# Two graph-attention layers on one core: half of a block's product moved into the next block's sums, and a GpSimd memset between two gathers

## The chip, the core and the metric

The kernel runs on one core of one Trainium2 chip. The metric is the device time of one execution in microseconds (us); the time before is a median of three runs. A profile is a separate execution, in which the hardware profiler records every instruction; its times are read against each other, and its span is longer than the timed runs.

## What is computed

The input is a matrix `x` of 2708 nodes by 1024 features and an adjacency matrix `adj` of 2708 x 2708 with few ones in a row (the kernel keeps at most 40 neighbours of a node). Two attention layers follow each other, each with a residual and a layer norm. Layer 0 scores a pair of nodes by a product of two projections, layer 1 by the sum of two numbers of the nodes:

```python
# layer 1; x is the output of layer 0
h = x @ W
f1 = h @ a1
f2 = h @ a2
e = leaky_relu(f1 + f2.T, negative_slope=0.2)
scores = where(adj > 0, e, -9e15)
attention = softmax(scores, axis=1)
x = layernorm(x + relu(attention @ h), axis=-1)
```

All of it is in float32.

## The kernel before

*Lists, not matrices.* A first stage turns each row of `adj` into a list of neighbours (`lists`, L402 on), sorts the nodes by the length of their lists and makes 22 blocks of them: one of 20 nodes, and 21 of 128 nodes each, a block being four groups of 32 nodes. A group with lists of up to 4 T entries has T *tiles*: a tile is 128 rows of 1024 features (in layer 1 and its ring, 1028: one more column holds a score), four neighbours of each of 32 nodes, fetched from memory by one indirect DMA, a *gather*, which GpSimd issues. There are 405 tiles in a layer; the first block has 3, most of the others 20.

*The order of layer 1.* `(attention @ x) @ W` is computed instead of `attention @ (x @ W)`. For each block `b` the loop at L1007 writes down, in this order:
- the copies (ScalarE) of the last block's turned rows, `yT`;
- the **sums** of block `b` (L679): for every tile, two matmuls (one for each half of 512 columns) add weighted rows into the PSUM tile `po`; four matmuls on the four column groups of the array run side by side. `st` holds the weights. When both halves of a tile are done, its slot is free and `gathers()` (L642) issues the next gathers, in program order, for as long as freed slots allow. At the end ScalarE copies `po`, divided by the row sums `ri`, into `y`;
- the **product** of block `b - 1` (`product`, L533): 16 matmuls `yT @ M`, 8 for each half of 512 columns, into the PSUM tile `pm`. In the records each matmul of float32 is two, so a product has 32;
- eight transposes (`turn`, L515) of `y` of block `b`, into the PSUM tile `pt`;
- the **close** of block `b - 2` (`close1`, L994): VectorE reads `pm`, adds the residual, and takes the norm; ScalarE applies it; GpSimd scatters the rows to the output (from a hook inside the next sums);
- the **scores** of block `b + 1` (`scores1`, L976): VectorE adds the column of scores in the gathered tiles to a number of each node, takes the maximum, ScalarE the exponential, and VectorE spreads the result into `st`.

*What holds the order.* Every engine gets its instructions through `InOrder` (L61), which keeps them in the order in which the program writes them; engines wait for each other by semaphores only.

*Buffers.* Gathered tiles live in a ring of 32 slots (20 in `ring`, 12 in `more`), so a gather waits until the tile 32 places earlier has been summed. `pm` has two buffers, `po` one, `y` and `yT` one each. A gather also waits for the eighth GpSimd DMA before it, since these share eight semaphores.

The helpers record all these operations under L71, so the groups are told apart by their tiles.

Of the kernel before, what the change touches and what calls it, by code (L numbers as in the profile page):

```python
# [8 lines left out]
F32 = mybir.dt.float32  # L9
# [97 lines left out]
def listed_path(ctx, tc, x, adj, Wf, bf, Wg, bg, W, bW, W1, a1, a2, out):  # L107

    nc = tc.nc
    P = 128  # L110
    N, D = x.shape
    KC = D // P
    H = D // 512
    TW = D + 4
# [6 lines left out]
    start = [0] + [valid[0] + P * b for b in range(NB - 1)]  # L121
# [11 lines left out]
    pe, dve, act, pool, sp = (InOrder(tc, e) for e in (nc.tensor, nc.vector, nc.scalar, nc.gpsimd, nc.sync))  # L133
# [5 lines left out]
    ps_m = ctx.enter_context(tc.tile_pool(name="ps_m", bufs=2, space=bass.MemoryType.PSUM))  # L139
# [3 lines left out]
    T1 = dram.tile([N, TW], F32, name="T1")  # L143
# [6 lines left out]
    ones3 = const.tile([35, P], BF16, name="ones3")  # L150
# [23 lines left out]
    rows3 = const.tile([35, D], BF16, name="rows3")  # L174
# [5 lines left out]
    def gather(engine, dst, table, idx, rows=N):  # L180
        engine.indirect_dma_start(
            out=dst, out_offset=None, in_=table,
            in_offset=bass.IndirectOffsetOnAxis(ap=idx, axis=0), bounds_check=rows - 1, oob_is_err=False)
# [3 lines left out]
    M = wm.tile([P, KC, D], F32, name="M")  # L187
# [6 lines left out]
    with tc.tile_pool(name="pre", bufs=1) as pre:  # L194
# [292 lines left out]
        for b in range(NB):  # L487
            n = nsize[b]
            pe.matmul(pt[:64, 0, :NG], low4[:n, b].rearrange("p j i -> p (j i)"), hot[:n, b, :],
                             start=(b == 0), stop=(b == NB - 1))  # L490
# [42 lines left out]
    def product(n, xT, w, row=None):  # L533


        pm = ps_m.tile([P, H, 512], F32, name="pm")
        for h in range(H):
            c = slice(h * 512, (h + 1) * 512)
            if row is not None:
                pe.matmul(pm[:n, h, :], ones3[row:row + 3, :n], rows3[row:row + 3, c], start=True, stop=False)  # L540
            for k in range(KC):
                pe.matmul(pm[:n, h, :], xT[:, k, :n], w[:, k, c],
                          start=(row is None and k == 0), stop=(k == KC - 1))
        return pm

    def split_product(xT, w, parts, row=None):

# [78 lines left out]
    class Layer:  # L626

        def __init__(self, units, rings, width, table, stp):  # L630
            self.units, self.table, self.width, self.stp = units, table, width, stp
            self.slots = [(t, i) for t in rings for i in range(t.shape[1])]
            self.count = len(self.slots)
            self.order = [(u, g, t) for u in units for _, g, t in u.tiles]
            assert self.count <= sum(TILES[:NSL0])
            self.next, self.free, self.most = 0, set(), len(self.order)
# [5 lines left out]
        def gathers(self):  # L642
            while self.next < min(self.most, len(self.order)) and (self.next < self.count or self.next - self.count in self.free):
                u, g, t = self.order[self.next]
                idx = SL[:, g, t:t + 1] if self.next >= self.count else SL0[:, g, t:t + 1]
                gather(pool, self.rows(self.next), self.table, idx)
                self.next += 1

        def soft(self, u):
# [93 lines left out]
    ring = ctx.enter_context(tc.tile_pool(name="ring", bufs=1)).tile([P, R0, TW], F32, name="ring")  # L743
    with ExitStack() as s0s:
# [3 lines left out]
        stp, xp, yp, jp = (new_pool(n, 1) for n in ("stp0", "xp", "yp", "jp0"))  # L748
        zs = new_pool("zp", 1).tile([P, TW], F32, name="z")
        seq = [1, 0, *range(2, NB)]  # L750
        units = cut(R0, 2, seq)
        lay = Layer(units, [ring], D, x, stp)
# [124 lines left out]
        closing, loaded = iter(()), None  # L877
# [77 lines left out]
    with ExitStack() as s1s:  # L955
        new_pool = lambda name, bufs: s1s.enter_context(tc.tile_pool(name=name, bufs=bufs))
        tp, yp, zp, ovp = (new_pool(n, 1) for n in ("tp1", "yp1", "zp1", "ovp"))
        stp = new_pool("stp1", 2)

        x1 = [rb, u1b]  # L960
        z1 = [u2b, zp.tile([P, D], F32, name="z1")]
        more = new_pool("ring1", 1).tile([P, R1 - R0, TW], F32, name="more")
        units = cut(R1, Q, range(NB))
        lay = Layer(units, [ring, more], TW, T1[:, :], stp)
        prod, yTs, y = {}, {}, {}


        fq = ovp.tile([P, NB, Q], F32, name="fq")
        f1q = ovp.tile([P, NB, Q], F32, name="f1q")
        dve.tensor_tensor(fq, f1.unsqueeze(2).to_broadcast([P, NB, Q]), quad.unsqueeze(1).to_broadcast([P, NB, Q]),  # L970
                          op=ALU.mult)
        pt = ps_t.tile([P, 4, P], F32, name="pt")
        pe.matmul(pt[:, 0, :Q * NB], rep, fq.rearrange("p b q -> p (b q)"), start=True, stop=True)
        dve.tensor_copy(f1q.rearrange("p b q -> p (b q)"), pt[:, 0, :Q * NB])

        def scores1(u):  # L976
            for k, g in enumerate(u.gs):
                at = [lay.slots[(u.at + m) % lay.count] for m, tile in enumerate(u.tiles) if tile[0] == k]
                t0 = 0
                while t0 < len(at):  # L980

                    t, s = at[t0]
                    step = at[t0 + 1][1] - s if t0 + 1 < len(at) and at[t0 + 1][0] is t else 0
                    c = 1
                    while step > 0 and t0 + c < len(at) and at[t0 + c][0] is t and at[t0 + c][1] == s + c * step:
                        c += 1
                    dve.tensor_scalar(u.sc[:, k, t0:t0 + c], t[:, s:s + (c - 1) * step + 1:max(step, 1), D],
                                      f1q[:, u.b, k:k + 1], None, op0=ALU.add)
                    t0 += c
            dve.scalar_tensor_tensor(u.sc, u.sc, SLOPE, u.sc, op0=ALU.mult, op1=ALU.max)  # L990
            dve.tensor_add(u.sc, u.sc, masked(u))
            lay.soft(u)

        def close1(b):  # L994
            m, xt, z = valid[b], x1[b % 2], z1[b % 2]
            sp.dma_start(xt[:m], X1S[start[b]:start[b] + m, :])
            dve.scalar_tensor_tensor(z[:m], flat(prod.pop(b))[:m], 0.0, xt[:m], op0=ALU.max, op1=ALU.add)
            for _ in norm(z, m):
                pass
            yield  # L1000
            scatter(out, ids[:m, b:b + 1], z[:m])

        lay.gathers()
        scores1(units[0])
        closing = iter(())
        waiting = []
        for k, u in enumerate(units):  # L1007
            nxt = units[k + 1] if k + 1 < len(units) else None
            b = u.b
            back = b - 1 if b > 0 else None  # L1010
            po = ps_s.tile([P, H, 512], F32, name="po")
            y[b] = yp.tile([P, D], F32, name="y1")
            if back is not None:
                for _ in yTs[back][1]:
                    pass
            lay.sums(u, po, {6: [lambda s=closing: [None for _ in s]]}, y[b])
            closing = iter(())
            if back is not None:
                if back > 0:
                    prod[back] = product(P, yTs.pop(back)[0], M)  # L1020
                else:
                    prod[back] = whole(split_product(yTs.pop(back)[0], M, z1[1]))
            yT = tp.tile([P, KC, P], F32, name="yT")
            steps = turn(y.pop(b), nrows[b], yT, halves=True)
            next(steps)
            yTs[b] = yT, steps
            if waiting:
                closing = close1(waiting.pop())
                next(closing)
            if back is not None:  # L1030
                waiting.append(back)
            if nxt is not None:
                scores1(nxt)
        for _ in closing:
            pass
        b = NB - 1
        for _ in yTs[b][1]:
            pass
        prod[b] = product(nrows[b], yTs.pop(b)[0], M)
        for b in waiting + [b]:  # L1040
            for _ in close1(b):
                pass


        over = ovp.tile([P, NG, QT], F32, name="over")
        pool.memset(over, 0.0)
        for g in range(1, NG):
            if TILES[g] < QT:
                pool.memset(over[:, g, TILES[g]:], 1.0)
        for q in range(Q):  # L1050
            pool.memset(over[32 * q:32 * q + valid[0], 0, TILES[0]:], 1.0)
        dve.scalar_tensor_tensor(over, SL, float(N), over, op0=ALU.is_lt, op1=ALU.mult)
        dve.tensor_reduce(bad[:, 0:1], over, AX.XY, ALU.add)
        dve.tensor_reduce(bad[:, 0:1], bad, AX.X, ALU.add)
        pt = ps_t.tile([P, 4, P], F32, name="pt")
        pe.matmul(pt[0:1, 0, 0:1], bad[:, 0:1], ones, start=True, stop=True)
        act.copy(flag, pt[0:1, 0, 0:1])
# [365 lines left out]
```

## Time and profile before

The time before is 1823.62 us (1822.46 to 1825.52). The profiled execution has a span of 2002.7 us.

| In the profile | busy us, or number | share of the span |
|---|---|---|
| TensorE (PE), matmuls | 1664.6 | 83% |
| VectorE (DVE) | 1174.9 | 59% |
| ScalarE (ACT) | 634.7 | 32% |
| GpSimd (POOL) | 1191.8 | 60% |
| gathers of layer 1 into `ring` | 260, mean 1003 ns | 260.9 us busy |
| gathers of layer 1 into `more` | 145, mean 1005 ns | 145.7 us busy |
| records of products `pm<-M,yT` | 704, mean 661 ns | 361.9 us busy |
| records of sums `po<-ring,st` and `po<-more,st` | 2660 and 580 | 346.7 and 88.2 us busy |

How to read it: a row of an engine is the time in which it executes something, not the time in which it is needed. A line of a timeline gives the start, the duration, the engine, the source line, the operation with its tile names (output `<-` inputs), the count, and in brackets how long the engine was idle before it and what released it; "issue" stands for nothing that the profile shows, "remote" for a releaser that it can't name. Columns of a table by stage are the stage, its length, the busy time (and number of instructions) of each engine, then the granted clock of TensorE as a share of full speed, the busy share of the 16 DMA engines, and the rate in GB/s.

The first gather of layer 1 starts at 1244.74 us of the span. In the 100 us from 1600 on TensorE is busy for 82.95 us and GpSimd for 62.41; the mean over the whole span hides that the stages differ.

### The profile page before, as it was taken

The page shows a single profiled execution, that of the slowest core. Times are in us where ns is not written, and L with a number is a line of the kernel's source. Part 1 is how long each engine was busy: PE and PEld are TensorE (multiplying, and loading weights), DVE is VectorE, ACT ScalarE, POOL GpSimd, SP SyncE. Part 2 cuts the span into 40 slices and gives each one's busy share as a digit, 9 for nine tenths or more (in the row PEclk, how much of TensorE's full clock was granted, in tenths as well). Part 3 has the DMA queues.
Part 4 walks back from the last instruction along what each step waited for, and adds up shares of the span by engine and source line. Part 5 has one row for each costly group of instructions (what it writes and reads, how often), then busy time and mean ns, then how long its engine had stood idle before and what let it go on. Part 6 is the DMA issues. An engine that isn't in the chain of part 4 may idle for free. (4 is left out here: it accounts for less than half of the span.)

```text
span 2002.7 us, 22908 instructions
## 1 busy us (share of the span) xinstructions
PE 1664.6 (83%) x7313; PEld 683.8 (34%) x7313; DVE 1174.9 (59%) x3541; ACT 634.7 (32%) x857; POOL 1191.8 (60%) x1191
## 2 busy tenths in 40 slices
PE   5998556899999889999999975468788888887985
PEld 3443222333344333443434432123233333332332
DVE  5879465788888678888888863123232323232332
ACT  4546134444554444445554440011010101011111
POOL 6978445666676456665666531755656565766621
PEclk9999677999999899999999988688889888998988
DMA  6644354656778567876777753887889889998830
GB/s 262 240 170 176 119 220 164 228 199 242 268 285 299 207 226 256 291 258 243 279 277 272 270 215 114 351 298 269 319 300 328 297 306 318 337 330 317 297 145 33
DMA packets 149982, 501.85 MB, mean 251 GB/s; under 512 B 32566, under 2 KB 32598, under 8 KB 147145
## 3 DMA queue, kind: packets, MB, share of 16 engines
q0 software_dynamic: 132032, 427.36, 59.7%
q1 hardware_dynamic: 10202, 55.72, 7.5%
q10 hardware_dynamic: 7618, 17.23, 2.4%
q8 instruction: 59, 0.97, 0.2%
q14 instruction: 71, 0.57, 0.1%
HBM read 509.64 MB, written 33.75 MB: 271 GB/s over the span
## 5 line engine op out<-in xcount | busy, mean ns | idle before, releaser
L71 POOL DMA_INDIRECT ring<-in_x_dram,SL x405 | 437.2, 1079 | 318.6 <-issue 97.0
L71 DVE SCALAR_TENSOR_TENSOR j<-ring,Fr 128x1024 bf16<-128x1024 f32 x402 | 494.8, 1231 | 89.4 <-DMA ring<-in_x_dram,SL 60.2
L71 PE MATMUL pm<-M,yT 128*128 128x512 f32 (+1 forms) x704 | 361.9, 661 | 85.7 <-issue 84.5
L71 POOL DMA_INDIRECT ring<-T,SL x260 | 260.9, 1003 | 166.3 <-issue 58.8
L71 PE MATMUL po<-ring,st 128*32 128x512 f32 x2660 | 346.7, 619 | 6.3 <-issue 6.2
L71 ACT COPY Fr<-pm 32x1024 f32<-32x1024 f32 (+1 forms) x349 | 338.4, 970 | 27.1 <-issue 16.3
L71 PE MATMUL pm<-M,xT 128*128 128x512 f32 (+1 forms) x704 | 316.5, 614 | 16.2 <-issue 15.8
L71 PE MATMUL pm<-Wt,xT 128*128 128x512 f32 (+1 forms) x704 | 309.3, 606 | 1.7 <-issue 1.6
L71 PEld LDWEIGHTS pm<-M,yT 128*128 128x128 f32 (+1 forms) x704 | 138.7, 202 | 301.3 <-issue 300.5
L71 ACT ACTIVATE y<-po,ri 128x512 f32<-128x512 f32 (+1 forms) x88 | 55.9, 684 | 569.3 <-remote 529.3
L71 POOL DMA_INDIRECT more<-T,SL x145 | 145.7, 1005 | 78.4 <-issue 37.8
L71 PEld LDWEIGHTS pm<-M,xT 128*128 128x128 f32 (+1 forms) x704 | 128.6, 191 | 184.2 <-issue 183.6
L71 PEld LDWEIGHTS pm<-Wt,xT 128*128 128x128 f32 (+1 forms) x704 | 126.7, 189 | 157.9 <-issue 157.7
L71 PEld LDWEIGHTS po<-ring,st 128*32 128x32 f32 x2660 | 100.1, 114 | 203.5 <-issue 201.6
L409 POOL TENSOR_TENSOR adj<-adj,iota 128x2708 f32<-128x2708 f32 (+3 forms) x23 | 130.6, 5682 | 28.6 <-ACT adj L71 28.5
L71 DVE TENSOR_TENSOR st<-scores,stack 128x384 f32<-128x384 f32 (+9 forms) x74 | 36.1, 521 | 186.6 <-ACT scores L71 93.0
L71 ACT ACTIVATE scores<-scores 128x24 f32<-128x24 f32 (+5 forms) x44 | 9.6, 219 | 423.0 <-DVE scores L71 253.4
L412 DVE MAX8 cand<-adj 128x8 f32<-128x136 f32 (+2 forms) x440 | 96.6, 284 | 40.3 <-POOL adj L409 40.3
L71 PE MATMUL pm<-halfT,WfT 128*128 128x512 f32 x256 | 113.7, 599 | 0.9 <-ACT WfT L71 0.9
L71 DVE TENSOR_SCALAR scores<-ring,f1q 128x2 f32<-128x2 f32 (+5 forms) x98 | 21.3, 235 | 140.3 <-DMA ring<-T,SL 126.2
L71 POOL DMA_INDIRECT SL<-LD,idq x85 | 87.5, 1030 | 25.8 <-issue 23.9
L71 PE MATMUL po<-more,st 128*32 128x512 f32 x580 | 88.2, 617 | 0.0
(199 smaller groups left out, 1412.3 us busy)
## 6 DMA issues: line engine op xcount, KB each, us to landing
adj<-in_adj_dram SPq DMA_DIRECT2D x21, 1354.0 KB
X1S<-z SPq DMA_DIRECT2D x20, 512.0 KB
ring<-in_x_dram,SL POOLq DMA_INDIRECT x405
u1b<-X1S SPq DMA_DIRECT2D x11, 512.0 KB
rb<-X1S SPq DMA_DIRECT2D x10, 512.0 KB
ring<-T,SL POOLq DMA_INDIRECT x260
rows<-in_L_gnn_Wg_dram ACTq DMA_DIRECT2D x8, 512.0 KB
rows<-in_L_gnn_Wf_dram ACTq DMA_DIRECT2D x8, 512.0 KB
```

The source lines that it names most:

```text
L71: made = self.tc.keep_in_program_order(op(*args, **kwargs))
L409: nc.gpsimd.tensor_tensor(k[:n, cut], k[:n, cut], iota[:n, cut], op=ALU.mult)
L412: nc.vector.max(cand[:n, s, :], k[:n, s * SEG:min((s + 1) * SEG, N)])
```

## The change

Two edits, both in layer 1.

The first takes the matmuls of one half of a product out of `product` into `half_product`. In layer 1 the first half of the product of block `b - 1` is now written down inside the sums of block `b`, behind half of its tiles; the second half follows the sums, where the whole product was. It is meant to spread the freeing of ring slots. Block 0's product, which is split in another way, stays whole.

The second gives the layer a scratch tile `space` of 128 x 192, and GpSimd writes zeros into it behind every gather of the layer, 405 times. Nothing reads it. It is meant to space the gathers.

```diff
         pm = ps_m.tile([P, H, 512], F32, name="pm")
         for h in range(H):
-            c = slice(h * 512, (h + 1) * 512)
...
-            for k in range(KC):
-                pe.matmul(pm[:n, h, :], xT[:, k, :n], w[:, k, c],
-                          start=(row is None and k == 0), stop=(k == KC - 1))
+            half_product(pm, h, n, xT, w, row)
         return pm
...
                 gather(pool, self.rows(self.next), self.table, idx)
+                if self.space is not None:
+                    pool.memset(self.space, 0.0)
                 self.next += 1
...
-        lay = Layer(units, [ring, more], TW, T1[:, :], stp)
+        lay = Layer(units, [ring, more], TW, T1[:, :], stp, ovp.tile([P, 192], F32, name="space"))
...
-            lay.sums(u, po, {6: [lambda s=closing: [None for _ in s]]}, y[b])
+            hooks = {6: [lambda s=closing: [None for _ in s]]}
+            if back is not None and back > 0:
+
+                xT, pm = yTs.pop(back)[0], ps_m.tile([P, H, 512], F32, name="pm")
+                prod[back] = pm
+                hooks.setdefault(len(u.tiles) // 2, []).append(lambda: half_product(pm, 0, P, xT, M))
+            lay.sums(u, po, hooks, y[b])
             closing = iter(())
             if back is not None:
                 if back > 0:
-                    prod[back] = product(P, yTs.pop(back)[0], M)
+                    half_product(pm, 1, P, xT, M)
                 else:
                     prod[back] = whole(split_product(yTs.pop(back)[0], M, z1[1]))
```

More of the change, by code (lines that the diff above doesn't have):

```diff
@@ L537, in product, with half_product @@
         for h in range(H):
-            c = slice(h * 512, (h + 1) * 512)
-            if row is not None:
-                pe.matmul(pm[:n, h, :], ones3[row:row + 3, :n], rows3[row:row + 3, c], start=True, stop=False)
-            for k in range(KC):
-                pe.matmul(pm[:n, h, :], xT[:, k, :n], w[:, k, c],
-                          start=(row is None and k == 0), stop=(k == KC - 1))
-        return pm
+            half_product(pm, h, n, xT, w, row)
+        return pm
+    def half_product(pm, h, n, xT, w, row=None):
+        c = slice(h * 512, (h + 1) * 512)
+        if row is not None:
+            pe.matmul(pm[:n, h, :], ones3[row:row + 3, :n], rows3[row:row + 3, c], start=True, stop=False)
+        for k in range(KC):
+            pe.matmul(pm[:n, h, :], xT[:, k, :n], w[:, k, c],
+                      start=(row is None and k == 0), stop=(k == KC - 1))
     def split_product(xT, w, parts, row=None):
@@ L626, in listed_path, with __init__ @@
     class Layer:
-        def __init__(self, units, rings, width, table, stp):
+        def __init__(self, units, rings, width, table, stp, space=None):
+            self.space = space
             self.units, self.table, self.width, self.stp = units, table, width, stp
```

## The prediction

> **What bounds the kernel now.** I read the page for the share of each engine, then the stages, then layer 1 (from 1244.74 us on) block by block. Busy time by stage, columns as named in the second line:
>
> ```profile
> core 0: us, PE busy (x) PEld busy (x) DVE busy (x) ACT busy (x) POOL busy (x), PEclk, DMA share, GB/s
> ...
> 1600.00:1700.00 100.00, 82.95 (x400) 32.28 (x396) 29.75 (x125) 10.87 (x21) 62.41 (x63) 0.86 0.88 314
> 1918.80:1943.90 25.10, 24.49 (x119) 9.43 (x120) 9.15 (x40) 3.66 (x8) 1.29 (x1) 0.87 0.12 43
> ```
>
> In the middle of layer 1 (first row) TensorE is 83% busy at 0.86 clock while DMA is 88% busy. The second row is one late block, when no gather is left: TensorE is hardly idle. The timeline of TensorE shows what happens in a middle block:
>
> ```profile
> 1603.59 10.57 PE L71 MATMUL pm<-M,yT 128*128 128x512 f32 x24
> 1615.47 0.67 PE L71 MATMUL pm<-M,yT 128*128 128x512 f32 x1 [1.32 <-issue]
> 1617.59 0.74 PE L71 MATMUL pm<-M,yT 128*128 128x512 f32 x1 [1.44 <-issue]
> 1619.67 1.01 PE L71 MATMUL pm<-M,yT 128*128 128x512 f32 x1 [1.34 <-issue]
> ```
>
> The product runs 24 records in 10.57 us, and then one record every 2 us, although it waits for nothing that is shown. A product without gathers beside it (the one at 1929.32) takes 14.00 us for its 32 records; this one takes 22.8 (1603.59 to 1626.42). The same stretch in windows of 2 us:
>
> ```profile
> 1614.00:1616.00 2.00, 0.68 (x2) 0.19 (x1) 1.44 (x9) 0.00 (x0) 1.70 (x2) 1.00 1.04 335
> 1622.00:1624.00 2.00, 1.22 (x3) 0.46 (x3) 0.00 (x0) 0.00 (x0) 0.99 (x1) 0.50 1.03 422
> ```
>
> The slow stretch begins when DMA is full (share 1.04) and has halved the clock by its end (0.50). ScalarE and GpSimd come back with TensorE:
>
> ```profile
> 1625.39 1.27 ACT L71 ACTIVATE y<-po,ri 128x512 f32<-128x512 f32 x2 [30.22 <-remote]
> 1625.58 0.99 POOL L71 DMA_INDIRECT ring<-T,SL  x1 [1.82 <-remote]
> ```
>
> The sums that y reads had ended by 1603.6, so y is 22 us late.
>
> **Are these stalls in the timed runs?** The profiled execution lasts 2002.7 us, the timed ones 1823.6: 179 us less. A middle block takes 33.4 us in the profile (copies of yT begin at 1321.30 and 17 blocks later at 1889.98). Before layer 1 there is little to give back: between 350 and 1200 us TensorE is busy for 789 of 850 us (61 idle). So I take most of the 179 us to be these stalls: they belong to the profiled run, and a timed block is shorter. What bounds it then, for a block of 20 tiles:
> - GpSimd: gathers start every 1.30 us (0.99 busy and 0.30 between), a scatter takes 1.02 + 0.31: 20 x 1.30 + 1.33 = 27.3 us.
> - DMA: 20 x 128 x 4112 B, and 0.52 MB read and 0.52 MB written for the close, 11.6 MB; at the 422 GB/s of the busiest window, 27.4 us.
> - TensorE: product 14.0, sums 8.7 (1629.35 to 1638.16), transposes 1.0, row sums 0.3, waits about 0.7: 24.7 us.
>
> GpSimd and DMA set the pace together and TensorE has some 2.7 us to spare. Check by the whole: (33.4 - 27.4) x 17 = 102 us of the 179 come from middle blocks, and 77 from all the rest, which has about that much idle and slow-clock time.
>
> **What the Trainium skill says.** "DMA: Bandwidth & Descriptors", section Anatomy of one DMA — SWDGE, prices a GpSimd DMA at 2.0 us and its bytes at 436 GB/s: 1.21 us of movement for a gather, an estimate; the trace's 422 GB/s gives 1.25 and is used. "Perfetto Trace Analysis", section GPSIMD Engine Instruction, says to time GpSimd by the spacing of starts; the trace agrees that the duration misleads, 0.99 against 1.30. "TensorE: Matmul & The Clock Gate", Part 1, says that idleness halves the clock; the 0.50 above agrees. "NOTIFIC — the notification-queue block", section 7.1, says that a backed-up record path can stall an engine; that fits stalls of all engines in the profile alone, but no run here shows it.
>
> **The change, part by part.**
> *The memset.* 405 of them, one behind every gather of layer 1. These rows of GpSimd give sizes around 192 columns (mean ns last):
>
> ```profile
> masks.py:197 POOL MEMSET ident<- 128x128 f32 x1 | 0.2, 205 | 0.3 <-POOLq L1409 0.3
> L226 POOL MEMSET early<- 128x484 f32 x1 | 0.5, 492 | 0.0
> L71 POOL MEMSET over<- 128x850 f32 x1 | 0.8, 829 | 0.0
> ```
>
> (829 - 205) / (850 - 128) = 0.86 ns a column, so 192 columns take 205 + 64 x 0.86 = 260 ns. Whether that lengthens the 1.30 us is the main unknown. There is one memset between two gathers, in layer 0:
>
> ```profile
> 261.99 0.99 POOL L71 DMA_INDIRECT ring<-in_x_dram,SL  x1 [0.30 <-issue]
> 262.97 0.13 POOL L71 MEMSET z<- 128x4 f32 x1
> 263.29 1.68 POOL L71 DMA_INDIRECT SL<-LD,idq  x1 [0.19 <-issue]
> ```
>
> It starts where the gather ends and the next gather starts 1.30 us after the first, as ever: it lay in the gap of 0.30. A 260 ns memset fits there too. Low end: 1.30. High end, nothing hidden: 1.30 + 0.26 = 1.56. Between: if the 0.19 behind the memset is fixed, 0.99 + 0.26 + 0.19 = 1.44. I take 1.32 (gap 0.32 in this example, not 0.30). At that, GpSimd needs 20 x 1.32 + 1.33 = 27.7 us a block against 27.4 of DMA: 405 x 0.02 = 8 us if GpSimd alone sets the pace, 0 if DMA does; I take 6. Each memset also waits for the previous one, which ended a gather earlier; behind it only gathers and scatters are queued, and for those the scores on VectorE wait.
>
> *The half product.* The same 32 records, 14.0 us, in two parts of 7.0, one in the middle of the next sums. No work is added; the split has no cost of its own, since weights are loaded before each record anyway. It delays the second half of the sums, and the freeing of some 10 slots, by 7 us. By then 10 slots are free, which is 13 us of gathers, and the second half frees from 4.4 + 7.0 = 11.4 us on: GpSimd doesn't starve. Its PSUM buffer was last read by the close one block before, its yT was copied before the sums: no new wait. After the sums 7.0 us of product remain, which hide y (1.27 us). Cost 0, gain 0, since TensorE is not the bound. Sum: +6 us, 1823.6 + 6 = 1830.
>
> **The rivals.**
> *B, the memset is not hidden.* At 1.44 GpSimd needs 20 x 1.44 + 1.33 = 30.1 us a block, 2.7 over DMA; by 20 blocks +54 us, 1878; a little less where sums and ring hold GpSimd up anyway: 1872. At 1.56 it would be 405 x 0.26 = 105 us, 1929. For it: the spacing of gathers never falls under 1.30, so GpSimd is saturated. Against it: the example.
> *C, the stalls are partly real.* If a fifth of the 6 us a block is in timed runs too, spaced gathers and evenly freed slots take it away: 1.2 x 20 = 24 us, 1800. For it: stalls begin only where DMA is full, and all engines show them. Against: the 179 us. This rival is faster.
> *D, y is late in timed runs too.* If y came 22 us behind the sums, 7 us of product wouldn't cover it: 15 us a block, over 2100. The late block above (y at 1929.52, just behind its sums) speaks against it; I give it next to nothing, and count it in B.
>
> **How the numbers follow.** My case 0.40, B with D 0.27, C 0.33. My case spreads over 1818 to 1838: faster 0.07, same 0.14, slower 0.19. B is slower, C faster: faster 0.40, same 0.14, slower 0.46. The range goes down past C's middle to 1793 and up past B's to 1880; the unhidden 1.56 and a C of a third or more of the stalls stay outside.
>
> **What would show it.** Gathers that start 1.30 to 1.35 us apart with a memset of about 260 ns in the gap: my case; 1.44 or more: B. In the profile of the changed kernel the product of a block in two runs of about 7 us, the first without idle time. If the slow records vanish and the timed run drops with the profiled one, C; if the profiled span drops alone, the stalls were the profile's. I'd be wrong throughout if GpSimd waits for slots (PE po as its releaser) more than before, or if TensorE waits for y.

## The result, and the profile after

The time after is 1878.94 us (1874.87 to 1879.76), against 1823.04 (1822.0 to 1825.52) for the kernel before, taken alongside: a ratio of 1.030, with a 95% interval of 1.0282 to 1.0319. The change makes the kernel 56 us slower. The forecast was 1830.0 us with a range of 1793 to 1880. The range held the time, but only just, and the point was 49 us too low; run again on another chip, where the kernel before took 1826.42, the same kernel took 1885.30 us, outside the range.

One caution on the profile shown ahead of the prediction: it is not like the timed runs, 2002.7 us long where they took 1823.6. That is not the way of every profile: the one of the kernel after has a span of 1877.0 us, within 2 us of its timed runs. So below the kernel after is compared with a second profile of the same kernel before, 1826.9 us long, taken among the experiments.

The page of the kernel after: busy time, the shares of the chain that ended last, and rows of its list of groups (busy, mean ns of one, then the idle time of the engine before them):

```profile
PE 1597.3 (85%) x7313; PEld 667.7 (36%) x7313; DVE 1188.1 (63%) x3541; ACT 633.8 (34%) x857; POOL 1297.5 (69%) x1596
...
POOL 23%; PE 9%; issue 5%; DVE 4%; DMA 3%; POOLq 1%; ACT 1%; DVEq 0%; ACTq 0%
...
L71 PE MATMUL pm<-M,yT 128*128 128x512 f32 (+1 forms) x704 | 303.8, 598 | 0.3 <-ACT yT L71 0.3
L71 POOL DMA_INDIRECT ring<-T,SL x260 | 259.8, 999 | 51.0 <-issue 43.4
...
L71 POOL MEMSET space<- 128x192 f32 x405 | 111.3, 275 | 0.2
```

The memset takes 275 ns, close to the 260 of the prediction, and GpSimd is hardly ever idle before it (0.2 us in 405 times). In the chain that ended last GpSimd has 23% of the span. In the second profile of the kernel before it has 3%, and the landing of DMAs more:

```profile
DMA 15%; PE 14%; issue 5%; DVE 5%; POOL 3%; ACT 1%; POOLq 0%; ACTq 0%; DVEq 0%
```

The products' records have 598 ns each and no idle time to speak of (they had 661 ns, and 85.7 us of idle time, in the profile of 2002.7 us).

GpSimd's timeline in the middle of layer 1 (start, duration, and in brackets the idle time before), first of the kernel before in its second profile, then of the kernel after:

```profile
1500.92 0.99 POOL L71 DMA_INDIRECT more<-T,SL  x1 [0.30 <-issue]
1502.22 0.99 POOL L71 DMA_INDIRECT more<-T,SL  x1 [0.30 <-issue]
```

```profile
1503.48 1.00 POOL L71 DMA_INDIRECT ring<-T,SL  x1 [0.17 <-issue]
1504.48 0.27 POOL L71 MEMSET space<- 128x192 f32 x1
1504.92 1.00 POOL L71 DMA_INDIRECT ring<-T,SL  x1 [0.17 <-issue]
```

This is most of the result. A gather starts 1.44 us after the one before: 1.00 for the gather, 0.27 for the memset, and another 0.17 behind the memset for which the profile shows nothing. Before, the two gathers stood 1.30 apart. The median spacing over the layer is 1.434 us against 1.298, so 405 x 0.136 = 55 us come from the spacing; the time grew by 55.9.

There is a second, smaller part. Behind four of the gathers (the 87th, 188th, 289th and 390th) the next one starts only 3.26 to 3.28 us later. The second of these places:

```profile
1475.86 1.00 POOL L71 DMA_INDIRECT more<-T,SL  x1 [0.16 <-issue]
1476.85 0.28 POOL L71 MEMSET space<- 128x192 f32 x1
1479.12 0.99 POOL L71 DMA_INDIRECT more<-T,SL  x1 [1.99 <-issue]
```

The four add 7 us over the usual spacing; the second profile of the kernel before has one such pause, of 1.83 us, behind the 390th alone. From the first gather of the layer to the last it is 610.2 us after and 550.8 before, 59 us more: 55 from the spacing and the rest mainly from these pauses. What causes them was not traced.

TensorE in the same stretch:

```profile
1510.77 7.13 PE L71 MATMUL pm<-M,yT 128*128 128x512 f32 x16
1519.57 1.90 PE L71 MATMUL po<-ring,st 128*32 128x512 f32 x16
1521.40 7.13 PE L71 MATMUL pm<-M,yT 128*128 128x512 f32 x16
1528.37 1.04 PE L71 MATMUL pt<-ident,y 128*128 128x128 f32 x8
```

The product lies in two unbroken runs of 7.13 us, one in the middle of the sums and one behind them. ScalarE copies `y` from 1521.61 on, as soon as the sums have ended, and the second half of the product hides it. By stage, in the same columns as ahead of the prediction:

```profile
1600.00:1700.00 100.00, 84.97 (x440) 32.95 (x432) 33.38 (x126) 10.90 (x21) 86.34 (x136) 0.93 0.96 355
1300.00:1700.00 400.00, 337.88 (x1778) 130.23 (x1780) 142.84 (x564) 47.23 (x91) 346.98 (x540) 0.92 0.95 347
```

GpSimd's 86.34 us of 100 leave little but the pauses of 0.17 behind the memsets and one of the four longer ones; over the 400 us DMA is no longer full (0.95, where the kernel before has 0.99, shown below).

### The profile page after: what moved, and what is told of

It reads as the page before. It is cut to its first block, busy times and chain, and to the rows that moved or that the text cites. A ratio compares the mean times of both kernels' runs of the same rounds, so it can differ in the third digit from the quotient of the medians.

```text
span 1877.0 us, 23310 instructions
## 1 busy us (share of the span) xinstructions
PE 1597.3 (85%) x7313; PEld 667.7 (36%) x7313; DVE 1188.1 (63%) x3541; ACT 633.8 (34%) x857; POOL 1297.5 (69%) x1596
## 5 line engine op out<-in xcount | busy, mean ns | idle before, releaser
L71 PE MATMUL po<-ring,st 128*32 128x512 f32 x2660 | 351.3, 629 | 0.1
L71 PE MATMUL pm<-M,xT 128*128 128x512 f32 (+1 forms) x704 | 307.5, 605 | 0.0
L71 PE MATMUL pm<-M,yT 128*128 128x512 f32 (+1 forms) x704 | 303.8, 598 | 0.3 <-ACT yT L71 0.3
L71 PEld LDWEIGHTS pm<-M,yT 128*128 128x128 f32 (+1 forms) x704 | 125.6, 186 | 177.5 <-issue 176.9
L71 POOL DMA_INDIRECT more<-T,SL x145 | 144.7, 998 | 28.4 <-issue 27.6
L71 PE MATMUL pt<-rs,stack 128*32 128x1 f32 x680 | 14.3, 180 | 145.6 <-DVE rs L71 74.6
L71 POOL MEMSET space<- 128x192 f32 x405 | 111.3, 275 | 0.2
L71 POOL DMA_INDIRECT SL<-LD,idq x85 | 86.7, 1020 | 25.8 <-issue 21.5
```

Source lines behind the costliest of these rows:

```text
L71: made = self.tc.keep_in_program_order(op(*args, **kwargs))
```

## The experiments

The theory after the result: GpSimd sets the pace of layer 1, the memset lengthens the spacing by its own length and 0.17 us, less the gap of 0.30 that was there, and the half product does nothing. Rivals: the half product costs or gives something too; DMA, which is as full as GpSimd, sets the pace; the stalls of the first profile play a part.

**Each edit alone.** First the memset without the half product:

```diff
-        def __init__(self, units, rings, width, table, stp):
+        def __init__(self, units, rings, width, table, stp, space=None):
+            self.space = space
...
+                if self.space is not None:
+                    pool.memset(self.space, 0.0)
...
-        lay = Layer(units, [ring, more], TW, T1[:, :], stp)
+        lay = Layer(units, [ring, more], TW, T1[:, :], stp, ovp.tile([P, 192], F32, name="space"))
```

> The 192-column memset behind every gather of layer 1 alone, the product left whole. Theory 1 (GpSimd sets the pace of layer 1, and the memset lengthens the spacing of gathers from 1.30 to 1.44 us): the whole loss is here, 405 x 0.14 = 57 us, 1876 to 1880 us. Theory 2 (the half product in the sums holds up the freeing of slots, and the memset only adds to it): clearly under the 1879 of the full change, say 1850 or less.

Measured: 1885.32 us against 1824.5 on the same chip, ratio 1.0333 (1.0309 to 1.0357), spacing 1.434. Then the half product without the memset, which is the change but for one argument:

```diff
-        lay = Layer(units, [ring, more], TW, T1[:, :], stp, ovp.tile([P, 192], F32, name="space"))
+        lay = Layer(units, [ring, more], TW, T1[:, :], stp)
```

> The half product inside the sums alone, no memset. Theory 1: the same TensorE work off the path, 1823 us within 5, and a profiled span near 2000 us, with the slow records of products still there, because gathers start every 1.30 us as before. Theory 2: slower, 1840 or more. A third possibility: evenly freed slots help, 1810 or less.

Measured: 1827.24 us, ratio 1.0013 (0.9998 to 1.0027). The memset is the whole loss. The half product neither costs nor gives anything that can be told from nothing. GpSimd never waits long for a slot with it: between 1300 and 1700 us its waits for sums add up to some 5 us, the longest 1.5. The long profile that was expected here did not come: its span is 1823.4 us.

To see whether the half product takes some of the memset's loss back when both are there, the changed kernel was run once more, unedited, beside others.

> The full change once more, beside memset192 alone at a ratio of 1.0333 (1.0309 to 1.0357). If the half product does nothing, the ratio lies in that interval; if it gives something back when GpSimd is the bound, 1.030 or less.

Measured: 1885.30 us against 1826.42, ratio 1.0319 (1.0292 to 1.0345). That interval and the memset's alone overlap almost wholly: nothing measurable is given back.

**The size of the memset.** The same edit as in the first run, with 4, 96 and 384 columns in place of 192. Four columns are the size of the example on which the prediction rested.

> A memset of 4 columns instead of 192 behind every gather, the product left whole. Theory 1 with a fixed 0.17 us behind a memset: 1.00 + 0.12 + 0.17 = 1.29 us between gathers, no loss, 1823 us within 5; the number of instructions and waits is that of the 192-column version. If the instruction itself or its wait costs, and not its length, then near 1879.

> A memset of 96 columns, the product left whole. By the spacing seen with 4, 192 and 384 columns (gather 1.00, memset 0.12, 0.27 and 0.43, and 0.17 behind it) a memset of 96 takes 0.18 to 0.19 and the spacing is 1.35 to 1.36: 405 x 0.055 = 22 us, 1843 to 1850. If DMA had slack to give (a pace of its own over 1.30), less: 1835.

> A memset of 384 columns, the product left whole. Theory 1: memset 0.27 + 192 x 0.86 ns = 0.44 us, spacing 1.00 + 0.44 + 0.17 = 1.61, 0.31 over 1.30, 405 x 0.31 = 126 us: 1945 to 1950 us. If DMA or TensorE set the pace, the time would not follow the spacing in proportion: under 1920.

| columns | memset, us (median) | spacing of gathers, us (median) | 405 x (spacing - 1.298), us | time, less that of before on the same chip, us | ratio (95%) |
|---|---|---|---|---|---|
| none | | 1.298 | 0 | 0 | 1 |
| 4 | 0.126 | 1.300 | 1 | 7.4 | 1.0049 (1.0031 to 1.0067) |
| 96 | 0.192 | 1.354 | 23 | 25.8 | 1.0141 (1.0121 to 1.0161) |
| 192 | 0.272 | 1.434 | 55 | 60.8 | 1.0333 (1.0309 to 1.0357) |
| 384 | 0.432 | 1.594 | 120 | 118.8 | 1.0654 (1.0627 to 1.0680) |

GpSimd's timeline with 4 columns, and then with 384:

```profile
1410.17 1.00 POOL L71 DMA_INDIRECT more<-T,SL  x1 [0.19 <-issue]
1411.16 0.13 POOL L71 MEMSET space<- 128x4 f32 x1
1411.47 1.00 POOL L71 DMA_INDIRECT more<-T,SL  x1 [0.19 <-issue]
```

```profile
1499.24 1.00 POOL L71 DMA_INDIRECT more<-T,SL  x1 [0.16 <-issue]
1500.23 0.44 POOL L71 MEMSET space<- 128x384 f32 x1
1500.83 1.00 POOL L71 DMA_INDIRECT more<-T,SL  x1 [0.17 <-issue]
```

The idle time behind the memset is 0.16 to 0.19 in both, though one memset is more than three times as long as the other. From 96 columns on, spacing = 1.00 + memset + 0.16 gives 1.35, 1.43 and 1.59. So of the gap of 0.30 about 0.13 can be filled, and each nanosecond beyond that is paid 405 times. The 4-column run has as many memsets, with the same waits, as the 192-column one, so it is the length that costs and not the instruction as such. The three longer sizes came out within 6 us of the times expected for them. Even 4 columns are not quite free, and 1831.85 us is above what was expected: from the first gather's start to the last one's it is 559.0 us, against 550.8 without a memset. The median spacing is 1.300, so the 8 us come from single longer spacings, mainly from the four pauses named above. Every profile with a memset has them, behind the same four gathers, with 3.23 to 3.28 us from start to start whatever the memset's length. Without a memset the half product alone has one, behind the 188th (the 1.5 us named above); half the bytes, below, has none.

**Were the stalls there at all?** The kernel before, unedited, profiled a second time:

> The kernel before, profiled once more. If the long profiled execution of before (2002.7 us, slow records of products, y 22 us late) belongs to profiling this kernel, it comes again: span near 2000 us. If it was one disturbed execution, the span is near 1822 us, gathers run on without a pause at 1.30 us, and y starts right behind the sums.

Measured: 1829.08 us, span 1826.9. TensorE in a middle block, and the stage:

```profile
1521.22 14.00 PE L71 MATMUL pm<-M,yT 128*128 128x512 f32 x32
1535.06 1.04 PE L71 MATMUL pt<-ident,y 128*128 128x128 f32 x8
```

```profile
1300.00:1700.00 400.00, 364.36 (x1948) 149.47 (x1944) 151.01 (x628) 53.80 (x103) 306.32 (x307) 0.95 0.99 382
```

The product has its 32 records in 14.00 us without a stall, `y` starts at 1521.39, just behind its sums, and the clock is 0.95. DMA is full (0.99 over 400 us) and yet nothing stalls. GpSimd's 307 instructions at 1.30 us are 399 of the 400 us: it hardly rests. A middle block takes 27.6 us (the product before this one began at 1493.61).

**GpSimd or DMA?** Both are full in that row, and so the memset alone does not say which of them sets the pace of the kernel before. First half the bytes: gathers of 514 numbers in place of 1028, as many of them as before. The result is then not the layer's; the run serves for its time alone.

```diff
-                              self.rows(u.at + index[k, t])[:, h * 512:(h + 1) * 512],
+                              self.rows(u.at + index[k, t])[:, (h if self.width > 600 else 0) * 512:][:, :512],
...
-        lay = Layer(units, [ring, more], TW, T1[:, :], stp)
+        lay = Layer(units, [ring, more], TW // 2, T1.rearrange("n (h c) -> (n h) c", h=2)[:N], stp)
...
-                dve.tensor_scalar(u.sc[:, k, t0:t0 + c], t[:, s:s + (c - 1) * step + 1:max(step, 1), D],
+                dve.tensor_scalar(u.sc[:, k, t0:t0 + c], t[:, s:s + (c - 1) * step + 1:max(step, 1), 0],
```

> Layer 1's gathers fetch rows of 514 instead of 1028 numbers, and both halves of the sums read the same 512 columns; scores are read from another column. So the result is not the layer's, and each gather moves half the bytes with the same instruction. If GpSimd's issue sets the pace: spacing still 1.30 us, time 1815 to 1825 us (only landing gets shorter), DMA share about half. If DMA shares the bound, the time falls below 1810.

Measured: 1822.86 us against 1826.42, ratio 0.9981 (0.9964 to 0.9997), the spacing still 1.31:

```profile
1300.00:1700.00 400.00, 363.02 (x1971) 147.77 (x1973) 150.88 (x630) 52.63 (x103) 307.08 (x306) 0.95 0.70 208
```

DMA falls from 0.99 to 0.70 of its time (about half was expected; the rate does fall to 208 from 382 GB/s), and GpSimd issues as many DMAs as before (306 against 307). So GpSimd's issuing is enough to hold the time. That does not say that it is alone: with less to issue, DMA might hold it at the same place. The counterpart takes work from GpSimd and leaves the bytes: SyncE stores the output rows one after the other, in the sorted order, where GpSimd scattered them to their places.

```diff
-            scatter(out, ids[:m, b:b + 1], z[:m])
+            sp.dma_start(out[start[b]:start[b] + m, :], z[:m])
```

> The kernel before, but the rows of layer 1's output are stored by SyncE to consecutive rows instead of scattered by GpSimd (so the output's rows are in the sorted order, not the nodes' order). GpSimd loses one DMA of 1.33 us in each block, the bytes stay. If GpSimd's issuing alone sets the pace of layer 1: 20 x 1.33 = 27 us less, 1798 (1793 to 1803), gathers still 1.30 apart. If DMA sets it together with GpSimd, as the prediction said (27.4 us of bytes a block): the time stays within 5 us of the kernel before, and gathers come 1.33 or more apart.

> The same, with gathers of half the bytes as in half_bytes (not the layer's result). Both theories say 27 us less than the kernel before, some 1797, if TensorE and VectorE have that much to spare; should it come out clearly below the run with full gathers, the difference is what DMA holds up once GpSimd has less to do; should both stay at 1823, something that is neither GpSimd nor DMA sets the pace just below.

This pair ran on a chip on which the kernel before takes 2009.93 us (1975.18 to 2049.64, 43 runs), and gave 1992.05 and 1992.49, both within 1% of it. It says nothing on the question at 1823 us, but it shows the stalls of the first profile again. TensorE's timeline, the plain store with full gathers:

```profile
1509.27 1.53 PE L71 MATMUL pm<-M,yT 128*128 128x512 f32 x2 [0.81 <-issue]
1511.38 1.21 PE L71 MATMUL pm<-M,yT 128*128 128x512 f32 x1 [0.59 <-issue]
1512.77 1.01 PE L71 MATMUL pm<-M,yT 128*128 128x512 f32 x1 [0.18 <-issue]
```

There the timed runs of the kernel before are about as long as its first profile. And half the bytes do not help: 1992.49 against 1992.05, with DMA at 0.58 of its time in the profile from 1300 to 1700 us. Full DMA is not what these stalls need. Both kernels were then measured on other chips, where the kernel before took 1824.43 and 1823.69.

> The kernel of plain_store once more, on a chip on which the kernel before takes 1823 us (the first was measured where it took 2010). GpSimd's issuing alone sets the pace of layer 1: 20 x 1.33 = 27 us less, 1798 (1793 to 1803), gathers 1.30 apart in an unbroken row. DMA sets it together with GpSimd: within 5 us of the kernel before, and GpSimd pauses now and then for a transfer. Between the two: the rest of GpSimd's 27 us that DMA or TensorE takes back.

> Both at once: no scatter on GpSimd, and gathers of half the bytes (not the layer's result), on a chip on which the kernel before takes 1823 us. Half the bytes alone gave 1823 and no scatter alone 1824. If GpSimd and DMA set the pace together, each holding the time where the other was relieved, both together give 20 x 1.33 = 27 us less, some 1797 (1790 to 1805). If something third (TensorE's chain of sums, product and turned rows, or the wait of the scores for the last gather) holds it, the time stays within 5 us of the kernel before.

Measured: the plain store with full gathers 1824.14 us, ratio 0.9993 (0.9979 to 1.0008); with half the bytes as well 1805.23 us, ratio 0.9903 (0.9868 to 0.9937). The stage of the first, and then of the second:

```profile
1300.00:1700.00 400.00, 367.03 (x1997) 148.32 (x1990) 154.45 (x643) 53.43 (x101) 293.03 (x296) 0.95 1.00 387
```

```profile
1300.00:1700.00 400.00, 374.57 (x2104) 155.37 (x2106) 161.41 (x671) 56.09 (x109) 306.39 (x308) 0.98 0.77 223
```

Count the gathers in these 400 us. The kernel before has 292 (307 DMAs less 15 scatters), the plain store 296, both edits together 308. Relieved of its scatters, GpSimd issues hardly more gathers: it now rests for some 400 - 296 x 1.29 = 18 us, with waits of up to 2.8 us, while DMA stands at 1.00. Relieved of bytes alone, it has no time for more. Only both together let it go on at 1.30 without a rest, 308 gathers, and the time falls by 18 us (11 to 24 by the interval) of the 27 expected; why it is not all of them was not traced. From the first gather of the layer to the last it is 550.8 us before, 543.0 with the plain store and 527.5 with both. So in the kernel before GpSimd and DMA do set the pace together: each holds the time when the other alone is relieved.

## Why the prediction went as it did

*The step that failed* is the memset's, "A 260 ns memset fits there too", and the 1.32 us taken from it. The duration was about right (275 ns measured, 260 worked out), but the room was not. The spacing is 1.434, so the term of the sum was 405 x 0.136 = 55 us instead of 6. The example had it already: behind the 4-column memset 0.19 us of idle time were left, where 0.30 stood without one. If the memset had simply lain in the gap, 0.30 - 0.13 = 0.17 would be left, and that is what was read into it. But the same figures fit a pause of a fixed length behind the memset, and a single size can't tell the two apart. The runs with 96, 192 and 384 columns can: the pause stays at 0.16 to 0.17 as the memset grows.

Rival B had this very sum (0.99 + 0.26 + 0.19 = 1.44), and it was given 0.27 where my case had 0.40. That the range reached the measured time is owed to B alone, not to the case on which the point rested. B's 1878 beside the measured 1878.94 is in part luck: it did not have the four longer pauses, and the memset's loss in the other runs was 59 and 61 us, not 56. Its correction to 1872, for times at which sums or ring hold GpSimd up anyway, was not needed.

*GpSimd and DMA together* held. The prediction put 27.3 and 27.4 us a block for the two, and a middle block takes 27.6. Neither edit by itself moved the time by more than 0.2% (0.9981 and 0.9993), and both at once did (0.9903). So GpSimd had no slack into which the memset could go: time added to it is paid in full, as the 192 and 384 columns show. No run adds bytes, so the same is not shown for DMA. The Trainium skill's "Perfetto Trace Analysis", section Optimizing DMA Performance (What "DMA-bound" means), lists the DMA engines and the issuing sequencer as separate things to be bound on; this kernel is at both limits at once. The page's advice for both is large descriptors. For the issuing side the runs agree in so far as a row of 4112 bytes is issued no more slowly than one of 2056 (1.30 us apart against 1.31), so that halving the rows gained nothing there.

*The stalls.* The step "they belong to the profiled run" was right in its consequence (the second profile, as long as the timed runs, has none) and wrong in its reason. On one chip all the timed runs are about as long as the first profile, and profiles there show the same stalls, so profiling is not needed for them, nor the record path named in the prediction. All long runs of the record but the first profile come from that one chip; where the first profile was taken is not on record, so it may be the chip rather than a single execution that has them. Nor do they need full DMA: at 0.99 there were none, and at 0.58 they were there. "Before layer 1 there is little to give back" did not hold either: in the second profile the first gather of layer 1 starts at 1206.04 us, 39 earlier. What causes the stalls stays open, and so does what the change does to a run that has them, since it was not run on that chip.

*The half product* at a cost and gain of 0 held (1.0013, 0.9998 to 1.0027; two unbroken runs of 7.13 us; no wait for slots). TensorE was idle for 35.6 of the 400 us in the second profile, some 2.5 us a block, close to the 2.7 of the prediction (whose sums of 8.7 us ran from 1629.35 to 1638.16, which is 8.8). With that to spare, where its work lies was worth nothing. *Rival C* rested on stalls in the timed runs and fell with them. *Rival D* fell too: `y` starts 0.2 us after TensorE goes from the sums to the product, before the change (1521.39 against 1521.22) and after it (1521.61 against 1521.40).

## What to carry to other kernels

A gap between two instructions of a saturated engine is not free room: find out, with two or three sizes, how much of it a new instruction may fill, and multiply the rest by the count. Where two resources are full at once, relieving one alone can show nothing, so relieve the two together before calling one of them the bound. And compare the span of a profile with the timed runs before reading stalls out of it; when they differ by a tenth, take another profile.

## What was not expected of the hardware

- In these runs a gather starts 0.16 to 0.19 us after a memset ends, and 0.30 us after another gather ends; a memset behind a gather starts at once. So about 0.13 us of memset can lie between two gathers.
- With a memset behind each gather, GpSimd also pauses about 2 us four times in the layer, some 101 gathers apart, in every run with memsets of 4 to 384 columns; the cause is open.
- The issuing of a gather of 128 rows takes 1.30 us from start to start at 4112 bytes a row and 1.31 at 2056.
- DMA moved 382 to 387 GB/s at a busy share of 0.99 to 1.00 over 400 us, with TensorE's granted clock at 0.95 beside it (the kernel before and the plain store).
- The kernel before takes 1823 to 1826 us on the other chips of this study and 2010 on one, on which two kernels derived from it show the stalls above in their traces.
